# A twelve-stage decoder: the wide cross-attentions' probabilities transposed in 32x32 blocks on VectorE and through DRAM

## The chip, the cores and the metric

The kernel runs on one core of a Trainium2 chip. The metric is device time in microseconds. The three runs shown took 2095.0, 2093.63 and 2095.06 us; their median is 2095.0 us. An engine is named as in the profile: PE is TensorE, DVE VectorE, ACT ScalarE, POOL GpSimd, SP SyncE (here it only issues DMAs).

## The reference

The program is a decoder of four layers. Each layer adds an attention, a cross-attention to a context and a feed-forward block to x, each on a layer norm of x. The batch is 4, the sequence 256, the width 128; the context has 512 tokens of width 96. All of it is float32. The two cross-attentions of the first and the last layer (stages X0 and X3) are wide: 16 heads of 64 features. Cut to what matters, both compute

```python
q = split(x_norm @ Wq)            # (4, 16, 256, 64)
k, v = split(ctx @ Wk), split(ctx @ Wv)   # (4, 16, 512, 64)
p = softmax(q @ k.T * 64 ** -0.5)  # (4, 16, 256, 512)
x = x + merge(p @ v) @ Wo + b
```

X0 adds low-rank terms to its weights, and keeps the last 4 context tokens apart, with a softmax of their own. Its long softmax runs over the other 508. The other stages are a one-head attention, a small grouped attention with a mixture of experts (F0), three more attentions and cross-attentions, a gated feed-forward, a feed-forward with 4-bit rounding (ffn2), and at the end six layers of local attention with a feed-forward (F3).

## The kernel before, in words

The four batch elements are almost independent, so the stages of different batch elements overlap. A list `ORDER` says in which sequence the pieces of the stages are written down. The class `Flow` then makes the real order. Every step is an operation with an engine, a cost in us and a due-time offset (the tables `NET` and `LOCAL`), the buffers that it reads, writes or holds, and the steps that it needs. `Flow.order` is a list scheduler: at each turn it takes, among the operations that can start first, the one with the earliest due time, and so fixes the order of the instructions on each of the five engines. Buffers have a fixed number of slots (`Net.TILES`, all cut from one SBUF arena by `LAYOUT`), and eight PSUM banks. Where the plan has PE waiting over 0.7 us for a bank's work, it puts in filler transposes of the identity (`keep`), 0.7 of the gap at 0.11 us each. The offsets and the paces in these tables are plain numbers in the source; all of them differ between the two kernels, so that the order of all stages differs somewhat.

X0 and X3 are written by `cross_wide` (lines 623 to 646). Per batch element `pair_values` makes the values of all heads: 8 products `p_v` of 512 columns, copied out of PSUM alternately by DVE (`p_vout`) and ACT (`p_vout_a`). `causal_wide` (stage A2) uses `pair_values` too, with 4 products per batch element. Then `cross_pair` runs for each of 8 pairs of heads:

- `p_k`, `p_q`: keys and queries of the pair on PE, copied out on ACT (`p_kout`) and DVE (`p_qout`).
- For each half t of the 256 queries: `p_scores` (PE, two banks, one for each head e), and per head `p_max` (DVE, line 687), `p_exp` (ACT, line 689), `p_recip` (DVE, line 691) and `p_share` (POOL, line 694, division by the sum).
- For each half and head: `p_turn`, four 128x128 transposes on PE into a bank (line 413 is the helper that issues them), and a copy of the bank into the tile `pT`, on ACT for t = 0 (`p_pT_a`) and on DVE for t = 1 (`p_pT`). Line 418 is the helper of all these copies.
- `p_weigh`: 8 products of PE with the values, keys on the partitions, and `p_wout` (ACT).

After 8 pairs `pair_out` projects and adds to x. There are 2 stages x 4 batch elements x 8 pairs = 64 pairs, 128 halves and 256 groups of four transposes.

PE, DVE, ACT and POOL each run their instructions in the planned order. SP issues the weight loads (`fetch`) in its planned order; a load that must wait for its buffer holds back what stands behind it. The weights of F3 are issued by ACT.

Of the kernel before, what the change touches and what calls it, by code (L numbers as in the profile page):

```python
# [22 lines left out]
F32 = mybir.dt.float32  # L23
# [323 lines left out]
class Net:  # L347
# [11 lines left out]
        "im": (384, 1), "xin": (256, 2), "h": (256, 2), "h2T": (256, 2), "rtmp": (256, 3), "gates": (16, 2),  # L359
        "top": (16, 6), "tr": (2, 6), "ss": (16, 2), "qs": (48, 4), "row": (128, 3),  # L360
        "pad0": (256, 2), "pad8": (256, 2), "vs": (1040, 2), "vb": (576, 2),
# [4 lines left out]
    w4 xT kx qx nmx sums p pT big st mv rs xn  # L366
    """

    def __init__(self, ctx, d):
# [14 lines left out]
            ("bank", *LocalBlock.TILES), ("scores", "weigh"), PORT, after,  # L384
        )
        self.flow.keep = lambda b: self.transpose(b.t[:, :P], d.ident)
        self.n = 0
# [214 lines left out]
    def pair_values(self, b, w, src, reads, chunks):  # L602
# [3 lines left out]
        for h in range(2):  # L606
            for c in range(chunks):
# [5 lines left out]
                self.evac("p_vout_a" if c % 2 else "p_vout", lambda to=to, at=at: to.t[:, at : at + 512],  # L613
# [45 lines left out]
    def cross_pair(self, b, g, w, xT, v, vmade, vt, oT, n, image):  # L659
# [12 lines left out]
        nmx, sums, pT, halves = self.buf("nmx"), self.buf("sums"), self.buf("pT"), []  # L672
        for t in range(2):
# [8 lines left out]
            for e in range(2):  # L682
# [23 lines left out]
                tp, half = self.buf("bank"), Buffer()  # L706
                halves.append(half)

                def turn(cols=cols, tp=tp):
                    for c in range(4):  # L710
                        self.transpose(tp.t[:, c * P : (c + 1) * P], cols(lo=c * P, hi=(c + 1) * P))

                self.op("p_turn", turn, [prob], [tp], [pT, p])
                self.evac(
                    "p_pT" if t else "p_pT_a",
                    lambda e=e, t=t: pT.t.rearrange("p (e c q) -> p e c q", e=2, q=S)[:, e, :, t * P : (t + 1) * P],
                    lambda tp=tp: tp.t.rearrange("p (c q) -> p c q", q=P), [tp], [half], [pT],
                )
        po, out = self.buf("bank"), Buffer()

        def weigh():
            pT4 = pT.t.rearrange("p (e c q) -> p e c q", e=2, q=S)
            for c in range(4):
                for e in range(2):
                    self.mm(
                        po.t[64 * e : 64 * (e + 1), :S], v(c, (2 * g + e) * 64), pT4[:, e, c, :], c == 0, c == 3
                    )

        self.op("p_weigh", weigh, [*halves, *vmade], [po], [pT, *vt, oT])
        self.evac("p_wout", lambda: oT.t[:, g * S : (g + 1) * S], lambda: po.t[:, :S], [po], [out], [oT])  # L730
        return out

# [1546 lines left out]
def slots():  # L2279
    return {"bank": 8} | {k: n for t in (Net.TILES, LocalBlock.TILES) for k, (_, n) in t.items()}  # L2280
# [4 lines left out]
    "n_stats": ("DVE", 0.77, -12.92),  # L2285
    "n_stats4": ("DVE", 1.36, 286.90),
    "n_eps": ("DVE", 0.11, -13.72),
    "n_root": ("POOL", 0.74, 139.58),
    "n_scale": ("DVE", 0.55, -1.32),
    "n_scale4": ("DVE", 1.18, 108.13),  # L2290
    "n_turn": ("PE", 0.25, 1.55),
    "warm": ("PE", 0.1, -281.88),
    "load_a": ("SP", 0.8, -912.31),
    "load_x": ("SP", 0.55, -820.02),
    "load_low": ("SP", 0.3, -687.28),
    "load_ups": ("SP", 2.05, -698.37),
    "load_wk": ("SP", 1.55, -609.16),
    "load_ctx0": ("SP", 0.8, -534.64),
    "load_wv": ("SP", 1.55, -493.10),
    "load_wq": ("SP", 2.05, -382.27),  # L2300
    "load_ctx": ("SP", 0.8, -269.42),
    "load_rows": ("SP", 1.55, -258.50),
    "load_image": ("SP", 1.55, -199.31),
    "load_wo": ("SP", 2.05, -147.00),
    "load_mask": ("SP", 0.9, 29.11),
    "k_causal": ("POOL", 1.4, 36.07),
    "k_ident": ("DVE", 0.2, -1.98),
    "k_masks": ("POOL", 1.7, 18.24),
    "k_pads": ("POOL", 1.3, 6.33),
    "k_values": ("POOL", 2.4, -15.88),  # L2310
    "k_image": ("POOL", 1.3, -15.31),
    "k_pick": ("POOL", 3.1, 50.17),
    "n_out": ("ACT", 0.34, 4.37),
    "add": ("DVE", 0.45, 12.29),
    "fetch": ("SP", 0.3, -129.69),
    "h_qk": ("PE", 0.87, -14.62),
    "h_qkout": ("DVE", 0.82, -17.26),
    "h_v": ("PE", 0.7, -17.34),
    "h_vout": ("ACT", 0.4, -209.49),
    "h_scores": ("PE", 0.87, -365.48),  # L2320
    "h_max": ("DVE", 0.74, -137.84),
    "h_exp": ("ACT", 1.0, 8.08),
    "h_recip": ("DVE", 0.1, 26.91),
    "h_turn": ("PE", 0.45, -7.58),
    "h_pT": ("ACT", 0.56, -83.79),
    "h_weigh": ("PE", 0.9, 4.47),
    "h_add": ("DVE", 0.64, -161.75),
    "p_v": ("PE", 0.92, -1.50),
    "p_vout_a": ("ACT", 0.62, -51.76),
    "p_vout": ("DVE", 0.63, 9.55),  # L2330
    "p_out": ("PE", 3.8, -8.71),
    "p_k": ("PE", 0.86, -1.76),
    "p_kout": ("ACT", 0.61, -23.45),
    "p_kimg": ("POOL", 0.22, -160.23),
    "p_q": ("PE", 0.45, 0.36),
    "p_qout": ("DVE", 0.36, -5.17),
    "p_scores": ("PE", 0.86, -7.16),
    "p_max": ("DVE", 0.62, -0.59),
    "p_exp": ("ACT", 0.71, 8.17),
    "p_recip": ("DVE", 0.1, 2.43),  # L2340
    "p_share": ("POOL", 0.73, -151.14),
    "p_img": ("DVE", 0.13, -114.70),
    "p_turn": ("PE", 0.47, -12.59),
    "p_pT": ("DVE", 0.63, 7.21),
    "p_pT_a": ("ACT", 0.62, -130.20),
# [400 lines left out]
```

## Time and profile before

| | us |
|---|---|
| median of three runs | 2095.0 |
| profiled execution, first to last instruction (span) | 2090.2 |
| PE busy (PE's weight loads busy) | 2027.3 (1354.4) |
| DVE busy | 1620.6 |
| ACT busy | 1176.6 |
| POOL busy | 991.7 |
| DMA traffic, MB | 71.20 |

The page gives no other time for the profiled execution than its span; the runs' median is 4.8 us above it. The mean granted clock of TensorE is 0.989. Busy time is the union of an engine's instructions. Matmul records overlap, since the next one starts while the last is still in flight, so a busy PE isn't a PE at its peak, and the cost of one matmul in a row of them is the distance between starts. The time by stretch is the better view: X0 lies between 34 and 362 us, X3 between 931 and 1230 us, and F3 behind.

### The profile page before, as it was taken

To read this page: it belongs to the slowest core of one execution; us is meant where nothing else is said; L and a number is where in the kernel's file an instruction comes from. 1 tells how busy PE (TensorE), PEld (TensorE's weight loads), DVE (VectorE), ACT (ScalarE), POOL (GpSimd) and SP (SyncE) were. 2 spreads that over 40 slices of the span, in tenths; PEclk is the share of its full clock that TensorE was granted. 3 is DMA by queue.
4 is the path that set the end of the run, shared out by engine and by line. 5 is a ranking of instruction groups with operands and counts; after the bars stand their busy time and mean duration, and the time that the engine had idled before them with its cause. 6 is when DMAs were issued, how large, how long until landed. Compare 5 with 4: busy or idle time off the path is not lost.

```text
span 2090.2 us, 59652 instructions
## 1 busy us (share of the span) xinstructions
PE 2027.3 (97%) x24411; PEld 1354.4 (65%) x24411; DVE 1620.6 (78%) x4281; ACT 1176.6 (56%) x2668; POOL 991.7 (47%) x1155
## 2 busy tenths in 40 slices
PE   9999999999999998999999999999999999999998
PEld 5656676776675666666556656666666666566666
DVE  6676877698786769988886589789787797797882
ACT  4565636344536677666656555555655565556553
POOL 4343424231312236444474367557566575575660
PEclk8999999999999999999999999999999999999999
DMA  5000020111020000100000101121121021111101
GB/s 158 1 1 1 1 71 1 42 42 45 5 74 2 9 1 25 39 1 1 1 1 1 52 21 63 46 70 46 43 70 43 25 71 53 63 46 42 30 23 32
DMA packets 33328, 71.20 MB, mean 34 GB/s; under 512 B 5528, under 2 KB 17888, under 8 KB 33056
## 3 DMA queue, kind: packets, MB, share of 16 engines
q1 hardware_dynamic: 20816, 51.48, 8.4%
q10 hardware_dynamic: 12240, 15.91, 2.3%
q8 instruction: 193, 3.16, 0.6%
q14 instruction: 79, 0.65, 0.1%
HBM read 41.69 MB, written 0.52 MB: 20 GB/s over the span
## 4 chain that ended last, share of the span: by engine, by line
PE 70%; DVE 20%; POOL 5%; issue 3%; ACT 1%; DMA 0%; SPq 0%; POOLq 0%; ACTq 0%; DVEq 0%
PE bank L410 40%; PE bank L1844 17%; PE bank L413 9%; PE bank L2060 2%; DVE arena L1998 2%; DVE arena L2008 2%; DVE arena L2013 2%; POOL arena L2050 1%; POOL arena L2012 1%; DVE arena L1637 1%; POOL arena L2093 1%; PE bank L2134 1%; DVE arena L2101 1%; DVE arena L2103 1%; DVE arena L2033 1%
## 5 line engine op out<-in xcount | busy, mean ns | idle before, releaser
L410 PE MATMUL bank<-arena 128*64 128x256 f32 (+12 forms) x6824 | 853.9, 393 | 6.6 <-ACT arena L1558 2.6
L410 PEld LDWEIGHTS bank<-arena 128*128 128x128 f32 (+5 forms) x6824 | 530.3, 165 | 269.1 <-issue 91.1
L1844 PE MATMUL bank<-arena 64*64 64x32 f32 (+3 forms) x13584 | 651.0, 251 | 6.8 <-issue 3.8
L1844 PEld LDWEIGHTS bank<-arena 64*64 64x64 f32 (+2 forms) x13584 | 386.8, 127 | 208.6 <-issue 115.7
L418 ACT COPY arena<-bank 128x256 f32<-128x256 f32 (+4 forms) x586 | 269.7, 489 | 273.6 <-PE bank L410 183.9
L2012 POOL TENSOR_TENSOR arena<-arena 128x1024 f32<-128x1024 f32 x96 | 226.5, 2363 | 124.3 <-PE bank L1844 65.1
L694 POOL TENSOR_SCALAR arena<-arena 128x508 f32<-128x508 f32 (+1 forms) x256 | 175.7, 693 | 214.3 <-DVE arena L691 189.4
L413 PE MATMUL bank<-ident,arena 128*128 128x128 f32 (+1 forms) x1757 | 252.2, 279 | 18.3 <-DVE arena L457 7.3
L413 PEld LDWEIGHTS bank<-ident,arena 128*128 128x128 f32 (+1 forms) x1757 | 194.7, 141 | 116.1 <-issue 41.3
L689 ACT ACTIVATE arena<-bank,arena 128x508 f32<-128x508 f32 (+1 forms) x256 | 174.7, 690 | 74.7 <-DVE arena L687 41.7
L2050 POOL TENSOR_TENSOR arena<-arena 128x1024 f32<-128x1024 f32 x96 | 180.6, 1902 | 74.0 <-DVE arena L2034 74.0
L2006 ACT ACTIVATE arena<-bank 128x512 f32<-128x512 f32 x192 | 114.2, 602 | 135.6 <-PE bank L1844 108.3
L687 DVE TENSOR_REDUCE arena<-bank 128x1 f32<-128x508 f32 (+1 forms) x256 | 163.8, 676 | 21.5 <-PE bank L410 21.3
L993 ACT ACTIVATE arena<-bank 128x512 f32<-128x512 f32 (+1 forms) x256 | 125.3, 580 | 72.8 <-PE bank L410 71.4
L2008 DVE TENSOR_TENSOR arena<-bank,arena 128x512 f32<-128x512 f32 x192 | 127.7, 683 | 37.7 <-ACT arena L2006 35.2
L418 DVE COPY arena<-bank 128x512 f32<-128x512 f32 (+1 forms) x196 | 125.4, 665 | 39.3 <-PE bank L413 26.6
L1998 DVE TENSOR_TENSOR arena<-bank,arena 128x256 f32<-128x256 f32 x384 | 138.5, 411 | 1.4 <-ACT arena L2006 1.4
L2093 POOL TENSOR_TENSOR arena<-arena 128x1024 f32<-128x1024 f32 x48 | 91.3, 1902 | 99.7 <-ACT arena L2066 62.7
L970 DVE TENSOR_REDUCE arena<-bank 128x1 f32<-128x512 f32 (+2 forms) x256 | 116.2, 513 | 22.6 <-PE bank L410 22.1
L2066 ACT COPY arena<-bank 128x512 f32<-128x512 f32 x192 | 103.3, 603 | 30.5 <-PE bank L2060 30.5
L2060 PEld LDWEIGHTS bank<-ident,arena 128*128 128x128 f32 x768 | 88.1, 143 | 41.9 <-POOL arena L2050 23.4
L2060 PE MATMUL bank<-ident,arena 128*128 128x128 f32 x768 | 102.1, 279 | 13.3 <-POOL arena L2050 13.3
(228 smaller groups left out, 2417.3 us busy)
## 6 DMA issues: line engine op xcount, KB each, us to landing
arena<-arena SPq DMA_DIRECT2D x48, 384.0 KB, 3.8
arena<-in_f_w SPq DMA_DIRECT2D x24, 512.0 KB, 3.5
arena<-in_f_wqkv ACTq DMA_DIRECT2D x18, 512.0 KB, 6.8
arena<-arena SPq DMA_DIRECT2D x48, 128.0 KB, 2.7
arena<-in_f_wo ACTq DMA_DIRECT2D x6, 512.0 KB, 4.0
arena<-in_f_w ACTq DMA_DIRECT2D x6, 341.0 KB, 4.0
arena<-in_f_w ACTq DMA_DIRECT2D x6, 192.0 KB, 5.9
arena<-in_x_wq SPq DMA_DIRECT2D x2, 512.0 KB, 3.3
```

What stands on the lines that cost most here:

```text
L410: self.nc.tensor.matmul(out, lhsT, rhs, start=start, stop=stop)
L413: self.nc.tensor.transpose(out, in_, self.d.ident)
L418: return self.op(name, lambda: copy(out(), in_()), reads, writes, holds)
L687: self.op("p_max", lambda ps=ps, one=one: nc.vector.tensor_reduce(one(nmx), ps.t[:, :n], AX.X, ALU.max, negate=True), [ps], [most], [nmx])
L689: self.op("p_exp", lambda ps=ps, one=one, cols=cols: nc.scalar.activation(cols(), ps.t[:, :n], AF.Exp, bias=one(nmx), accum_out=one(sums)) ...
L694: nc.gpsimd.tensor_scalar(cols(), cols(), one(sums), 1.0, ALU.mult, ALU.mult)
L1844: self.nc.tensor.matmul(out, lhsT, rhs, start=start, stop=stop)
L1998: nc.vector.tensor_mul(heads(tmp.t[:, cut])[:, :, lo : lo + 32], heads(ps.t)[:, :, 32 - lo : 64 - lo], spread(1, lo, lo + 32),)
L2008: op("cosine", lambda cut=cut, ps=ps: nc.vector.tensor_mul(heads(out.t[:, cut]), heads(ps.t), spread(0, 0, 64)), [ps, w["tab"]], [out])
L2012: op("rotary", lambda: nc.gpsimd.tensor_add(out.t, out.t, tmp.t), [out, tmp], [out])
L2050: nc.gpsimd.tensor_mul(heads(out.t), heads(out.t), rs.t[:, at : at + 16, None].to_broadcast([P, 16, 64]))
L2060: nc.tensor.transpose(ps.t[:, i * P : (i + 1) * P], out.t[:, (g + i) * P : (g + i + 1) * P], d.ident)
```

## The change

In `cross_pair` the transposes on PE and the copies of their banks go. In their place:

- `p_turn` (now DVE, one per half, 128 in all): `nc.vector.transpose` of 128x1024 probabilities, both heads of a half. It transposes every 32x32 block in itself and writes the blocks in another order into a new tile `ts`. A block's keys then lie on 32 partitions, but on the 32 of the queries' block, not on their own.
- `p_send` (SP, one per pair): four DMAs of 32 partitions each, 256 KB, from `ts` into a room in DRAM, which put each row where it belongs.
- `p_move` (SP, one per pair): one DMA of 1 MB from the room back into `pT`.
- `p_weigh` reads `pT` by a strided pattern in runs of 32 elements.

There are three rooms in DRAM (`ROOMS`) and two `ts` tiles of 8 KB per partition. To make space, `xin` goes from two slots to one and `rtmp` from three to two (both are used by F0 alone). All value copies of `pair_values` go to ACT, those of A2 too. The planner counts 3.5 us from the end of `p_send`, and 6.0 us from the end of `p_move`, until their data have landed. All due-time offsets, both paces and both patiences are new; the costs of the steps that stay are the same.

```diff
-        "im": (384, 1), "xin": (256, 2), "h": (256, 2), "h2T": (256, 2), "rtmp": (256, 3), "gates": (16, 2),
+        "im": (384, 1), "xin": (256, 1), "h": (256, 2), "h2T": (256, 2), "rtmp": (256, 2), "gates": (16, 2),
...
+        "ts": (2048, 2), "pad0": (256, 2), "pad8": (256, 2), "vs": (1040, 2), "vb": (576, 2),
...
+        self.rooms = [dram.tile([P, 2048], F32, tag=f"room{i}", name=f"room{i}", bufs=1) for i in range(ROOMS)]
...
-                self.evac("p_vout_a" if c % 2 else "p_vout", lambda to=to, at=at: to.t[:, at : at + 512],
+                self.evac("p_vout_a", lambda to=to, at=at: to.t[:, at : at + 512],
...
-                tp, half = self.buf("bank"), Buffer()
-                halves.append(half)
-
-                def turn(cols=cols, tp=tp):
-                    for c in range(4):
-                        self.transpose(tp.t[:, c * P : (c + 1) * P], cols(lo=c * P, hi=(c + 1) * P))
-
-                self.op("p_turn", turn, [prob], [tp], [pT, p])
-                self.evac(
-                    "p_pT" if t else "p_pT_a",
-                    lambda e=e, t=t: pT.t.rearrange("p (e c q) -> p e c q", e=2, q=S)[:, e, :, t * P : (t + 1) * P],
-                    lambda tp=tp: tp.t.rearrange("p (c q) -> p c q", q=P), [tp], [half], [pT],
-                )
+                probs.append(prob)
+            turned.append(self.blocks_turned(p, ts, t, probs[-2:]))
+        self.blocks_moved(ts, turned, pT)
...
-            pT4 = pT.t.rearrange("p (e c q) -> p e c q", e=2, q=S)
+            pT4 = pT.t.rearrange("p (a t e c i) -> p e c t a i", a=4, t=2, e=2, c=4)
...
-        self.op("p_weigh", weigh, [*halves, *vmade], [po], [pT, *vt, oT])
+        self.op("p_weigh", weigh, [pT, *vmade], [po], [*vt, oT])
...
+    def blocks_turned(self, p, ts, t, reads):
+        nc, done = self.nc, Buffer()
+        self.op("p_turn", lambda: nc.vector.transpose(
+            ts.t.rearrange("p (m t x i) -> p t m x i", m=4, t=2, i=32)[:, t],
+            p.t.rearrange("p (x m i) -> p m x i", m=4, i=32)), reads, [done], [p, ts])
+        return done
+
+    def blocks_moved(self, ts, turned, pT):
+        nc, room, sent = self.nc, self.fixed("room", self.rooms), Buffer()
+
+        def send():
+            to, from_ = room.t.rearrange("(m j) (a x) -> a j m x", m=4, a=4), ts.t.rearrange("p (m x) -> p m x", m=4)
+            for a in range(4):
+                nc.sync.dma_start(out=to[a], in_=from_[32 * a : 32 * (a + 1)])
+
+        self.op("p_send", send, turned, [sent], [ts, room])
+        self.op("p_move", lambda: nc.sync.dma_start(out=pT.t, in_=room.t), [sent], [pT], [room])
...
-    "p_turn": ("PE", 0.47, -12.59),
-    "p_pT": ("DVE", 0.63, 7.21),
-    "p_pT_a": ("ACT", 0.62, -130.20),
-    "p_weigh": ("PE", 1.62, 27.56),
+    "p_turn": ("DVE", 1.17, -1174.67),
+    "p_send": ("SP", 2.2, -26.91),
+    "p_move": ("SP", 0.55, 962.30),
+    "p_weigh": ("PE", 1.62, 22.74),
...
-NET_PACE = 1.197514
-NET_PATIENCE = 10.319527
+NET_PACE = 1.220588
+NET_PATIENCE = 6.798603
...
-LOCAL_PACE = 1.123621
-LOCAL_PATIENCE = 0.000000
+LOCAL_PACE = 1.128757
+LOCAL_PATIENCE = 6.287785
...
-LAGS = {**{k: 2.0 for k in NET if k[:5] == "load_"}, "fetch": 6.0, "constants": 4.0, "weights": 12.0, "spread": 3.5}
+LAGS = {**{k: 2.0 for k in NET if k[:5] == "load_"}, "fetch": 6.0, "p_send": 3.5, "p_move": 6.0, "constants": 4.0, "weights": 12.0, "spread": 3.5}
...
+ROOMS = 3
```

## The prediction

> **What bounds the kernel now.** I read the page's busy times and slices first, then the busy time by stretch, then the time line of TensorE around the transposes, and last the groups by shape and the DMA issues.
>
> ```profile
> span 2090.2 us, 59652 instructions
> PE 2027.3 (97%) x24411; PEld 1354.4 (65%) x24411; DVE 1620.6 (78%) x4281; ACT 1176.6 (56%) x2668; POOL 991.7 (47%) x1155
> PE 70%; DVE 20%; POOL 5%; issue 3%; ACT 1%; DMA 0%; SPq 0%; POOLq 0%; ACTq 0%; DVEq 0%
> ```
>
> TensorE is busy nearly always and holds 70% of the chain that ended last; no DMA is on that chain. The first and the last row maximum of each wide cross-attention (line 687) start at 34.0 and 361 us and at 931 and 1229 us, so I cut the span there:
>
> ```profile
> 0.00:34.00 34.00, 29.89 (x132) 20.40 (x134) 16.36 (x47) 6.78 (x15) 15.77 (x43) 0.80 0.85 242
> 34.00:362.00 328.00, 328.00 (x2312) 214.47 (x2310) 237.65 (x775) 190.86 (x494) 130.11 (x336) 1.00 0.04 12
> 362.00:931.00 569.00, 555.54 (x5064) 382.72 (x5062) 450.17 (x1451) 320.42 (x873) 186.52 (x304) 1.00 0.08 26
> 931.00:1230.00 299.00, 291.51 (x1758) 180.99 (x1755) 239.04 (x617) 181.62 (x475) 142.21 (x185) 0.99 0.03 10
> ...
> 800.00:850.00 50.00, 44.91 (x339) 31.76 (x338) 46.99 (x161) 33.82 (x114) 29.03 (x44) 1.00 0.10 28
> ```
>
> After the stretch and its length the columns are PE, PEld, DVE, ACT, POOL, the clock, DMA share and GB/s. In both cross-attention stretches PE is full (328 of 328, 291.5 of 299) and DVE comes next with 238 and 239. The last line shows how full DVE gets anywhere here: 47.0 of 50, 0.94. DMA is almost unused there, 3 to 4%.
>
> ```profile
> 1143.13 1.47 PE L413 MATMUL bank<-ident,arena 128*128 128x128 f32 x12
> 1144.53 3.86 PE L410 MATMUL bank<-arena 64*128 64x512 f32 x24
> 1148.33 1.53 PE L413 MATMUL bank<-ident,arena 128*128 128x128 f32 x12
> 1149.79 0.48 PE L410 MATMUL bank<-arena 64*128 64x128 f32 x2
> ```
>
> Twelve transposes hold PE from 1143.13 to 1144.53 and twelve more from 1148.33 to 1149.79: 2.86 us for 24, a slot of 0.119 us each (the 279 ns of one is latency that the next overlaps).
>
> ```profile
> L418 DVE COPY arena<-bank 128x512 f32<-128x512 f32 x184 | 120.8, 682 | 37.6 <-PE bank L413 26.6 <-PE bank L410 10.3
> L2013 DVE TENSOR_REDUCE arena<-arena 128x16 f32<-128x1024 f32 x96 | 114.3, 1200 | 0.0
> L1506 DVE TENSOR_TENSOR arena<-arena 128x1024 f32<-128x1024 f32 x4 | 5.1, 1274 | 6.0 <-POOL arena L1505 6.0
> L2050 POOL TENSOR_TENSOR arena<-arena 128x1024 f32<-128x1024 f32 x96 | 180.6, 1902 | 74.0 <-DVE arena L2034 74.0
> arena<-arena SPq DMA_DIRECT2D x48, 384.0 KB, 3.8
> arena<-in_f_w SPq DMA_DIRECT2D x24, 512.0 KB, 3.5
> arena<-arena SPq DMA_DIRECT2D x48, 128.0 KB, 2.7
> arena<-in_ctx SPq DMA_DIRECT2D x4, 192.0 KB, 2.6
> ```
>
> These give the prices: a 128x512 copy out of PSUM costs DVE 120.8/184 = 0.657 us, a pass over 128x1024 in SBUF 1.2 us. A DMA needs 2.6 to 2.7 us when small, plus 2.9 us per MB (192 to 512 KB) or 4.3 us per MB (128 to 384 KB).
>
> **The change part by part.**
>
> *TensorE, removed.* 2 stages x 4 batches x 8 pairs x 4 groups of 4 transposes = 1024 slots of 0.119 = 122 us. The order of the instructions in the two built programs puts 124 of the 256 groups inside the first stretch and 122 inside the second: 59 and 58 us. So PE alone would need 328 - 59 = 269 and 299 - 58 = 241 us. The other 10 groups (5 us) lie where PE bounds too.
>
> *VectorE, removed and added.* The 128 copies p_pT go, and p_vout (40 of the 80 value copies, eight of them in A2) moves to ScalarE. By the order 62 + 12 = 74 and 60 + 13 = 73 copies leave the stretches: 48.6 and 48.0 us. 61 and 62 block turns come in. No row shows this operation. Its nearest rows are the reduction (1.2) and the two-input pass (1.27) over the same 128x1024 on the same engine; I take 1.2. The ends are 1.06 (ScalarE's exponential over 128x1024, line 2105) and 1.9 (the same size on POOL). DVE becomes 237.65 - 48.6 + 73.2 = 262 and 239.04 - 48.0 + 74.4 = 265 us. That is 97% of PE's 269 and more than PE's 241. At the 0.94 of the fullest slice the stretches need 279 and 282 us. **DVE takes over the bound in both**, and instead of 117 us they give back 627 - 561 = 66. What is late next there is the row maximum, so the scores wait for banks. With the turn at 1.06 they give 84, at 1.27 56.
>
> *Work moved by the new due times.* The order has 14 more p_v inside the two stretches and as many fewer outside (two matmul records of 0.46 us each, 0.92): 13 us of PE leave parts that PE bounds and enter stretches where PE now has room. The rest that moves is smaller (four expert passes, four projections of the last stage); I leave it at 0, bounds -10 and +10, as for the reordered start and last stage.
>
> *ScalarE* loses 128 copies and gains 40 of about 0.56 us (L418's rows there): 49 us less on an engine at 56 to 61%. Nothing, hidden beside PE and DVE; without that cover it would be a gain.
>
> *SP and DMA.* Per pair four sends of 256 KB to DRAM, then one 1 MB load back that waits for them: 320 issues of about 0.45 us, 144 us on SP, which computes nothing. 128 MB at the 285 GB/s of the start (242 at share 0.85) is 450 us of DMA in 561 us, beside compute. The trip: the sends 5 to 6.5 us, the load 5 to 6.5, in sum 10 to 13. What stands behind a waiting load on SP are next sends and the weights of F0 and A1, fetched ahead; a delay of some 5 us is hidden by that lead. The trip itself must be covered by PE's order. From the second p_scores of a pair to its p_weigh the order holds 17.8 us of PE work on average (14.9 to 35.8, mean 18.9 in stage 0; 11.2 to 30.8, mean 16.8 in stage 3; 12.7 on average before), in the code's cost per step, which where I compared fits the rows (p_max 0.62; three of line 687 take 1.86). The chain it covers is two maxima 1.24, exponential 0.9 (with reading its sum), reciprocal 0.15, share 0.7, turn 1.2, hand-overs 0.6, thus 4.8, plus the trip: 15 to 18. At 17 the pairs that are short add to 50 us; about 2.2 pairs are in flight and a pause counts for all of them, so 23 us of pauses. They lie inside the 51 us that PE idles anyway when DVE bounds, so they add 0 (0 to 20).
>
> *Fillers.* The order has 365 filler transposes against 210: 155 x 0.119 = 18 us, in those pauses: 0 in the sum, 18 if PE alone bounds.
>
> *Buffers.* xin goes from 2 to 1 and rtmp from 3 to 2, to make room. Each serves F0 alone; a later f_turns waits for a POOL addition of 0.8 us: 0 to 10 us, hidden under DVE's other work; I take 0. The strided right operand of p_weigh: 0 (to 10 us, 512 matmuls at 0.02).
>
> **Sum** against the profiled execution: -66 - 13 - 5 = -84, so a span of 2006. The runs' median, 2095.0, is 4.8 above the span of 2090.2; I leave that unchanged: **2011 us**.
>
> **A rule against the change.** The row says 0.119 us for a transpose on TensorE, and a DVE pass of 1024 elements 1.2 us. The Trainium skill, "VectorE: DVE Perf Modes", The three transpose paths, has 390 ns for a 128x128 bf16 transpose on TensorE and 311 ns on VectorE, and its rules for authors send a 128x128 transpose to TensorE where PSUM will do. By its 311 ns a turn of eight such tiles is an estimated 2.5 us, and the stretches would come out some 85 us longer than 645 us, thus slower. In streaming PE the row is a third of the page's figure, and a lone tile's price includes a start that one long instruction pays once, so I stay with the rows.
>
> **The rivals.**
> - *PE alone still ends it*: the work is mixed so well that DVE never holds PE. For it: PE still has more work than DVE over the first 1230 us (about 1110 against 980). Against it: the order moves little between stretches. -122 + 18 = -104: 1991.
> - *The trip is too long*: at 15 us instead of 12 (DMAs of SP queueing among themselves) the short pairs add to 185 us, 84 with 2.2 in flight: 510 + 84 = 594, -33 - 18 = -51: 2044. It would be slower only from about 17 us. Against it: the rows' 10 to 13.
> - *The turn is dear* (the other side): DVE without turns holds 380 us in the two stretches; 123 turns at x, over 0.94, reach the old 627 + 18 us at x = 1.84. At 1.9 it is 653: +8, 2103; at 2.36 (POOL's slowest 128x1024, line 2012) +68, 2163. For it: no row of this operation, and its output is strided. Against: DVE's two 128x1024 rows.
> - *Nothing changes* in the 4 us (0.2%) that a measurement of this kernel can tell: only by gain and turn cancelling near x = 1.84.
>
> **How the numbers follow.** Forecast 0.52 (its own range 1985 to 2040), PE alone 0.17, long trip 0.14 (a quarter of it past its turning point), dear turn 0.14, cancelled 0.03. Faster: 0.52 + 0.17 + 0.10 = 0.79; same 0.03; slower 0.04 + 0.14 = 0.18. The range goes from below the PE case (1991 less the 15 us of moved work) to the dear turn's near end: 1975 to 2100, with about 0.05 below and 0.14 above.
>
> **What would show it.** The helper's transposes on PE should fall by 1024 less the 155 fillers; DVE in the two stretches should be at 0.9 or more and PE at about 0.9; a turn should last 1.2 us; the load back should land in 5 to 6.5 us and PE's wait for it stay under 25 us. I am wrong if the turn is over 1.8 us, if PE's waits name the load, or if the middle and last stretches move by more than 20 us.

## The result, and the profile after

The changed kernel takes 2125.07 us (median of four runs, 2120.37 to 2128.79); the kernel before took 2094.32 us beside it. The ratio is 1.0161, with a 95% interval of 1.0136 to 1.0187: 1.6% slower, where 2011 us and a gain were forecast. The profiled execution took 2120.37 us, its span is 2118.6 us.

First the page of the changed kernel: span, PE's and DVE's busy time, and the chain of work that ended last.

```profile
span 2118.6 us, 58103 instructions
PE 1969.9 (93%) x23542; PEld 1265.3 (60%) x23542; DVE 1664.9 (79%) x4241; ACT 1133.6 (54%) x2580; POOL 993.0 (47%) x1155
PE 46%; DVE 29%; DMA 11%; POOL 5%; issue 4%; ACT 3%; SPq 2%; ACTq 0%; POOLq 0%; DVEq 0%
```

PE was relieved (97% before, 93% now), and DVE hasn't filled up in its place (79%). What is new is DMA with 11% of the chain, where it had 0%.

The stretches of the changed kernel, cut at the first and last row maximum of X0 and X3 (the columns are those of the prediction: stretch, length, PE, PEld, DVE, ACT, POOL, clock, DMA share, GB/s):

```profile
31.00:370.00 339.00, 308.48 (x1921) 181.91 (x1918) 264.56 (x768) 171.50 (x458) 130.25 (x335) 0.97 0.65 207
370.00:922.00 552.00, 533.17 (x4918) 363.00 (x4917) 437.23 (x1442) 316.24 (x865) 185.60 (x306) 0.99 0.10 33
922.00:1259.00 337.00, 288.30 (x1401) 149.66 (x1400) 276.68 (x617) 168.90 (x440) 151.27 (x188) 0.94 0.62 195
```

X0 went from 327 to 338 us and X3 from 297 to 336, from first to last maximum. Neither engine is full there: PE has 308 of 339 and 288 of 337, DVE 0.78 and 0.82. The middle got shorter (569 to 552). The span's 28.4 us are +11 in X0, +39 in X3, -17 in the middle, and -4 at the start and the end.

What PE, DVE and SP waited for in the changed kernel (us in total, times, longest; `room` is the DRAM buffer, line 745 the load back, 742 the sends, 730 the turn):

```profile
PE bank L412 <- DMA arena<-room: 63.0, 29, 8.2
PEld bank L412 <- DMA arena<-room: 26.8, 11, 4.1
DVE arena L730 <- DMA room<-arena: 18.1, 11, 4.7
SPq L745 <- DMA room<-arena: 263.3, 113, 7.2
```

PE stood 63.0 + 26.8 = 90 us at `p_weigh` for the load back. DVE stood 18 us because `ts` was not yet sent. SP stood 263 us at loads until their own sends had landed.

The turn, and the issues of the two DMA steps with KB each and the median us to landing:

```profile
L730 DVE STREAM_TRANSPOSE arena<-arena 128x1024 f32<-128x1024 f32 x128 | 157.0, 1234 | 20.5 <-DMA room<-arena 18.1
room<-arena SPq DMA_DIRECT2D x256, 256.0 KB, 6.5
arena<-room SPq DMA_DIRECT2D x64, 1024.0 KB, 6.3
```

SP's queue in X0 of the changed kernel, as a time line (start, us that the issues took, line):

```profile
66.06 0.34 SPq L745 DMA_DIRECT2D arena<-room  x1
66.45 2.52 SPq L742 DMA_DIRECT2D room<-arena  x4
74.80 0.34 SPq L745 DMA_DIRECT2D arena<-room  x1
75.18 2.51 SPq L742 DMA_DIRECT2D room<-arena  x4
83.85 0.34 SPq L745 DMA_DIRECT2D arena<-room  x1
```

Four sends take 2.5 us to issue (66.45 to 68.97), SP then waits 5.8 us until they have landed, issues the load at 74.80, and only then the sends of the next pair. One pair goes through in about 9 us, and while the load of one pair runs, the sends of the next run beside it.

Over all 64 pairs, the time from the second turn's end to the first send is 1.95 us on average (the sends stand behind the previous pair's waiting load), from the first send to the load's issue it is 8.42, and the load takes 6.3 (median): **the trip is 16.7 us**. The planner had counted on 2.2 + 3.5 + 0.55 + 6.0 = 12.25, I on 10 to 13.

### The profile page after: what moved, and what is told of

Its sections match the earlier page's. It is cut to its first block, busy times and chain, and to the rows that moved or that the text cites. A ratio compares the mean times of both kernels' runs of the same rounds, so it can differ in the third digit from the quotient of the medians.

```text
span 2118.6 us, 58103 instructions
## 1 busy us (share of the span) xinstructions
PE 1969.9 (93%) x23542; PEld 1265.3 (60%) x23542; DVE 1664.9 (79%) x4241; ACT 1133.6 (54%) x2580; POOL 993.0 (47%) x1155
## 4 chain that ended last, share of the span: by engine, by line
PE 46%; DVE 29%; DMA 11%; POOL 5%; issue 4%; ACT 3%; SPq 2%; ACTq 0%; POOLq 0%; DVEq 0%
PE bank L412 28%; PE bank L1858 11%; DMA room<-arena 6%; DMA arena<-room 4%; PE bank L415 4%; DVE arena L2012 3%; DVE arena L2022 3%; DVE arena L2027 3%; PE bank L2074 2%; DVE arena L730 2%; SPq L742 2%; DVE arena L690 2%; DVE arena L2117 2%; DVE arena L2115 2%; POOL arena L2064 1%
## 5 line engine op out<-in xcount | busy, mean ns | idle before, releaser
L412 PE MATMUL bank<-arena 128*128 128x128 f32 (+10 forms) x6824 | 885.2, 402 | 88.9 <-DMA arena<-room 63.0
L412 PEld LDWEIGHTS bank<-arena 32*128 32x128 f32 (+5 forms) x6824 | 536.8, 167 | 384.3 <-issue 137.3
L1858 PE MATMUL bank<-arena 64*64 64x32 f32 (+2 forms) x13584 | 647.7, 250 | 14.1 <-issue 9.0
L1858 PEld LDWEIGHTS bank<-arena 64*64 64x64 f32 (+2 forms) x13584 | 382.1, 126 | 204.5 <-issue 130.9
L420 ACT COPY arena<-bank 128x256 f32<-128x256 f32 (+3 forms) x498 | 224.4, 472 | 315.1 <-PE bank L412 271.8
L730 DVE STREAM_TRANSPOSE arena<-arena 128x1024 f32<-128x1024 f32 x128 | 157.0, 1234 | 20.5 <-DMA room<-arena 18.1
L415 PE MATMUL bank<-ident,arena 128*128 128x128 f32 (+2 forms) x733 | 126.5, 288 | 19.1 <-POOL arena L1656 6.2
L415 PEld LDWEIGHTS bank<-ident,arena 128*128 128x128 f32 (+2 forms) x733 | 83.0, 143 | 82.8 <-issue 19.3
L2027 DVE TENSOR_REDUCE arena<-arena 128x16 f32<-128x1024 f32 x96 | 114.8, 1206 | 0.2
```

The source lines that it names most:

```text
L412: self.nc.tensor.matmul(out, lhsT, rhs, start=start, stop=stop)
L415: self.nc.tensor.transpose(out, in_, self.d.ident)
L420: return self.op(name, lambda: copy(out(), in_()), reads, writes, holds)
L730: self.op("p_turn", lambda: nc.vector.transpose(ts.t.rearrange("p (m t x i) -> p t m x i", m=4, t=2, i=32)[:, t], p.t.rearrange("p (x m i) ...
L1858: self.nc.tensor.matmul(out, lhsT, rhs, start=start, stop=stop)
L2027: op("norms", lambda: nc.vector.tensor_reduce(ss.t[:, at : at + 16], heads(sq.t), AX.X, ALU.add), [sq], [ss])
```

## The experiments

Three theories were set against each other: the trip theory (PE waits because the trip through DRAM is too long, by its bytes or by its latency), the DVE theory (the forecast's: DVE bounds the two stages), and the order theory (the new due times cost the time). "X0 + X3" below is the sum of both stages from first to last row maximum: 624.6 us before, 674.2 in the changed kernel. A pair's *cover* is the PE work that the order holds from its second scores to its weighing. A pair's *chain* is what the cover has to hide, from the first row maximum of its second half to the landed load.

### The same DMAs with 32 columns each

```diff
-                nc.sync.dma_start(out=to[a], in_=from_[32 * a : 32 * (a + 1)])
+                nc.sync.dma_start(out=to[a][:, :, :32], in_=from_[32 * a : 32 * (a + 1), :, :32])
-        self.op("p_move", lambda: nc.sync.dma_start(out=pT.t, in_=room.t), [sent], [pT], [room])
+        self.op("p_move", lambda: nc.sync.dma_start(out=pT.t[:, :32], in_=room.t[:, :32]), [sent], [pT], [room])
```

> The changed kernel in its own order, with the same 320 DMAs, but each send and each load back carries 32 columns instead of 512 or 2048, so nearly no bytes (most of the probabilities aren't moved, so the output is left incomplete; the two pT tiles are cleared once at the start). Trip theory (PE waits for the way through DRAM, about 14.8 us from the first send to the landed load): the trip falls to about 7 us, PE's 90 us of waits on the load vanish, the two stretches go from 676 to about 565 us, and the time is 2010 to 2030 us. DVE theory (the forecast's: DVE bounds the stretches): DVE's work is unchanged, the stretches stay near 676 us, 2110 to 2125. Order theory (the new due times cost it): 2110 to 2125 too.

Measured: 2035.86 us, ratio to before 0.9732 (0.9713 to 0.9752). No wait of PE names the room. The two stretches of this run:

```profile
34.00:336.00 302.00, 299.82 (x1927) 176.55 (x1924) 264.15 (x768) 171.18 (x458) 130.22 (x335) 1.00 0.13 35
885.00:1178.00 293.00, 278.69 (x1416) 143.81 (x1416) 274.71 (x615) 168.25 (x442) 149.78 (x187) 0.98 0.11 24
```

The order, the instructions and the buffers are those of the changed kernel; 89 us are gone, and of the 83 us by which the profiled span fell, 80 are in X0 (301) and X3 (293). DVE has the same work as in the changed kernel (264 and 275 us), so neither DVE nor the order as such explains the loss. X0 is now full on PE (300 of 302) and X3 has DVE at 275 of 293, the 0.94 of the forecast.

The edit takes away more than the bytes, though. The 32 columns belong to the pair's first half alone, so the sends no longer stand behind the second turn: in 62 of 64 pairs they start before it has ended, in the changed kernel in none. The trip cost 89 us in this order, by its bytes and by its place behind the second turn together.

### Half of the bytes

```diff
-            for a in range(4):
+            for a in range(2):
-        self.op("p_move", lambda: nc.sync.dma_start(out=pT.t, in_=room.t), [sent], [pT], [room])
+        self.op("p_move", lambda: nc.sync.dma_start(out=pT.t[:, :1024], in_=room.t[:, :1024]), [sent], [pT], [room])
```

> The changed kernel in its own order, with two sends of 256 KB and a load of 512 KB per pair (half of the probabilities aren't moved; the pT tiles are cleared once). Trip theory, by bytes: the DMA rings are shared by one pair's send and the last pair's load, 2 MB per 8.5 us; with half the bytes the send lands in 4 to 5 instead of 6.5 us and the load in 4 to 4.5 instead of 6.3, trip about 9.5 us, time 2030 to 2060. Trip theory, by latency (a landing takes its 6 us whatever it carries): send and load land in 5.5 to 6.5 us each, time 2095 to 2115. DVE theory: 2110 to 2125.

Measured: 2033.07 us, ratio 0.9719 (0.97 to 0.9739); X0 + X3 592.5 us. Sends land in 3.6 us, loads in 3.9, and the load is issued 4.9 us after the first send on average: a trip of 8.8 us, and nothing is left of the loss. Here every pair's sends still stand behind its second turn, as in the changed kernel, so the length of the trip is enough to explain the loss. The cost isn't in proportion to the bytes. Somewhere between a trip of 8.8 and one of 16.7 us it begins.

### Longer trip in the plan

```diff
-"p_send": 3.5, "p_move": 6.0,
+"p_send": 6.4, "p_move": 6.4,
```

> The changed kernel, but the planner is told of the measured landings (6.4 us each instead of 3.5 and 6.0), so that it puts more PE work between a pair's scores and its p_weigh. Order theory in the form that the plan only misjudged the trip: PE's waits on the load go from 90 to under 30 us and the time to 2060 to 2085. Trip theory by bytes: two tiles of each kind and the shared rings still allow a pair only every 8.7 us, so the waits move to other places and the time stays within 2100 to 2125. DVE theory: no change, 2115 to 2125.

Measured: 2120.42 us, ratio 1.0123 (1.0097 to 1.0148). X0 + X3 fell by 31 us to 643.2, and PE's wait from 90 to 68 us, but X3's end to the end of the kernel took 889 us instead of 860, and the middle 561 instead of 552. PE's and SP's waits for the trip:

```profile
PE bank L412 <- DMA arena<-room: 42.2, 24, 2.9
PEld bank L412 <- DMA arena<-room: 25.3, 12, 3.2
SPq L745 <- DMA room<-arena: 40.7, 24, 4.9
```

By the total the new plan seemed worthless; by the stages it helped where it should, and the other stages came out longer. The reading is that the list scheduler, whose due times were fitted to the old lags, put them in a worse order; the runs with due times fitted anew, below, bear on that. The new plan also changed SP's order: 52 of the 64 loads now stand behind a later pair's sends, where 8 did, and SP's wait at the loads fell from 263 to 41 us. The trip got no shorter by it (0.04 + 10.45 + 8.06 = 18.5 us, the same three parts as above), and PE still waited.

### Without DRAM: 16 DMAs per pair from SBUF to SBUF

```diff
             for a in range(4):
-                nc.sync.dma_start(out=to[a], in_=from_[32 * a : 32 * (a + 1)])
-
-        self.op("p_send", send, turned, [sent], [ts, room])
-        self.op("p_move", lambda: nc.sync.dma_start(out=pT.t, in_=room.t), [sent], [pT], [room])
+                for m in range(4):
+                    nc.sync.dma_start(
+                        out=pT.t[32 * m : 32 * (m + 1), a * 512 : (a + 1) * 512],
+                        in_=ts.t[32 * a : 32 * (a + 1), m * 512 : (m + 1) * 512],
+                    )
+
+        self.op("p_send", send, turned, [pT], [ts])
...
-    "p_send": ("SP", 2.2, -26.91),
-    "p_move": ("SP", 0.55, 962.30),
+    "p_send": ("SP", 7.2, -26.91),
...
-"p_send": 3.5, "p_move": 6.0,
+"p_send": 2.5,
```

> The blocks go from SBUF to SBUF in one hop: 16 DMAs of 64 KB per pair straight into pT, no DRAM, no second DMA, half the bytes; the planner counts 7.2 us of issue and 2.5 us to landing. Trip theory: the trip is 16 issues of 0.45 = 7.2 plus a landing of 2.3 to 2.7, thus 9.5 to 10 us instead of 14.8; the time is 2020 to 2060. DVE theory: 2110 to 2125. If SP's issue rate binds instead (16 x 0.45 x 32 = 230 us per stretch, or 0.65 to 1.2 each under load as some sends show), 2060 to 2110.

Measured: 2258.8 us, ratio 1.0793 (1.0769 to 1.0818). The DMA issues, and PE's first wait:

```profile
arena<-arena SPq DMA_DIRECT2D x1024, 64.0 KB, 2.0
```

```profile
PE bank L412 <- DMA arena<-arena: 143.8, 48, 5.7
```

Half of the bytes and a landing of 2.0 us, and yet the slowest of all: 16 issues in a row take SP 10.4 us, 0.65 us each, more than a pair's share of a stage (X0's 301 us without trip / 32 = 9.4). Between one pair's last issue and the next pair's first there are 0.11 us (median), and SP's queue holds 19% of the chain that ended last: the trip is bound by its issues here. That is a miss of mine (0.45 us each was assumed), and it says nothing on DRAM itself. A second thing differs: with a trip of 9.7 us in the plan the order holds only 15.0 us of cover per pair, less than any other run with all pairs moved, and the two causes aren't separated.

### Every second pair by the old way

```diff
+                if g % 2:
+                    tp, half = self.buf("bank"), Buffer()
+                    halves.append(half)
...
+                    self.op("p_tturn", turn, [prob], [tp], [pT, p])
...
-        self.blocks_moved(ts, turned, pT)
+        if not g % 2:
+            self.blocks_moved(ts, turned, pT)
...
+    "p_tturn": ("PE", 0.47, -12.59),
+    "p_pT": ("DVE", 0.63, 7.21),
+    "p_pT_a": ("ACT", 0.62, -130.20),
```

> Every second pair goes the old way (transposes on PE, copies on ACT and DVE with the costs and due offsets of before), the others the new way, so the bytes of the trips halve and each trip has two pairs' time. Trip theory: the waits of PE for the load fall from 90 us to under 20; PE has 61 us more of transposes than with all pairs moved, DVE 64 turns less (79 us) and 64 copies more (42 us). Without the bytes the kernel took 2036 us with DVE at 0.94 in X3 and PE full in X0; with half of the transposes back on PE I expect 2040 to 2060, faster than before. DVE theory (the turn is what costs): DVE's work falls by 37 us, so at most that much of 2125 is gained: about 2090. Order theory (the new due times cost the time): little changes, 2100 to 2125.

Measured: 2115.76 us, ratio 1.0116 (1.0093 to 1.0139). PE waits 1.3 us for the load. X0 + X3 is 630.7 us, 43 less than in the changed kernel and 6 more than before, but from X3's end to the kernel's end it takes 898 us (2107.9 - 1210), where the changed kernel has 860:

```profile
1210.00:2300.00 1090.00, 845.62 (x15333) 577.73 (x15328) 676.96 (x1388) 469.97 (x803) 514.29 (x288) 0.99 0.14 39
```

The two stages lost the wait, and the rest came out longer, as in the run with the longer trip planned.

### The load back issued by ScalarE's queue

```diff
-        self.op("p_move", lambda: nc.sync.dma_start(out=pT.t, in_=room.t), [sent], [pT], [room])
+        self.op("p_move", lambda: nc.scalar.dma_start(out=pT.t, in_=room.t), [sent], [pT], [room])
...
-    "p_move": ("SP", 0.55, 962.30),
+    "p_move": ("ACT", 0.55, 962.30),
...
-"p_send": 3.5, "p_move": 6.0,
+"p_send": 6.4, "p_move": 6.4,
```

> The load back is issued from ScalarE's queue instead of SyncE's, with 6.4 us planned for the sends and for the load, so that no send and no weight load stands behind a waiting load on SyncE. If the bytes on the DMA rings make the trip long, it stays at 2100 to 2125 us, as with the same planned times on SyncE (2120), with some us more for ScalarE's waiting at the loads. If it is the waiting on SyncE that holds the next pair's sends back, sends and loads overlap more and it comes to 2060 to 2090.

Measured: 2096.14 us, ratio 1.0031 (1.0011 to 1.0051). The total lies between the two expectations, so the stages have to decide. Against the run with the same planned times on SP it is 24 us less, but X0 + X3 is 651.8 instead of 643.2: the gain lies in the other stages' order (854 us from X3's end instead of 889, the middle 553 instead of 561). A queue of its own for the load did not make the two stages shorter. PE's wait for the load fell (44 us against 68), but now ScalarE's exponentials (line 692) stood behind loads that waited for their sends:

```profile
ACT arena L692 <- DMA room<-arena: 39.1, 9, 8.0
```

### A turn of a quarter of the size, with the 32-column trip

```diff
-            ts.t.rearrange("p (m t x i) -> p t m x i", m=4, t=2, i=32)[:, t],
-            p.t.rearrange("p (x m i) -> p m x i", m=4, i=32)), reads, [done], [p, ts])
+            ts.t.rearrange("p (m t x i) -> p t m x i", m=4, t=2, i=32)[:, t, :, :2],
+            p.t.rearrange("p (x m i) -> p m x i", m=4, i=32)[:, :, :2]), reads, [done], [p, ts])
```

> As the run with 32 columns per DMA, but the block turn also covers only a quarter (128 x 256 of 128 x 1024); the rest of the turned tile is left as it is, so most of the turning and moving is left out. A turn should fall from 1.23 to about 0.4 us, DVE's work in each stretch by some 50 us. If DVE bounded X3 there (275 us of work in 293, 0.94) and PE bounded X0 (300 of 302), X3 falls to 265 to 280 (then PE ends it) and X0 stays at 295 to 301; the whole 2010 to 2030 us. If DVE bounds both, both fall by over 15 us. If neither, both stay within 4 us, and 2036 stays.

Measured: 2024.2 us, ratio 0.9677 (0.9644 to 0.971); a turn takes 0.432 us. The two stretches of this run:

```profile
34.00:332.00 298.00, 296.93 (x1916) 174.37 (x1913) 216.58 (x765) 170.37 (x456) 129.55 (x334) 1.00 0.14 35
882.00:1167.00 285.00, 273.06 (x1404) 141.39 (x1403) 231.40 (x616) 168.36 (x441) 149.57 (x188) 0.99 0.11 24
```

DVE has 48 and 43 us less to do, X0 falls by 3.0 us (300.7 to 297.7) and X3 by 9.0 (293.2 to 284.2), less than the 13 or more that were expected. So PE bounds X0. In X3 DVE was the bound at 0.94, but PE stood 9 us behind it.

### The new order with the old transposes

```diff
-            turned.append(self.blocks_turned(p, ts, t, probs[-2:]))
-        self.blocks_moved(ts, turned, pT)
+                    self.op("p_tturn", turn, [prob], [tp], [pT, p])
+                    self.evac(
+                        "p_pT" if t else "p_pT_a",
...
```

> The due times, paces, buffers and ScalarE's value copies of the changed kernel, but every pair transposed on PE and copied as before (costs and due offsets of those steps as before): no turn and no trip. It shows what the new order costs or gives by itself. Trip theory: as before or somewhat better, 2075 to 2100, since the stretches outside of X0 and X3 were 17 us shorter in the changed kernel and this remains. Order theory: the new due times hold the 30 us that the changed kernel lost, so 2115 to 2130.

Measured: 2140.12 us, ratio 1.0242 (1.0211 to 1.0273), slower than both kernels, with X0 + X3 at 650.4 us and 891 us from X3's end to the kernel's end (861 before, 860 in the changed kernel). Taken alone it would speak for the order theory. But the 32-column run and the half-of-the-bytes run have the changed kernel's very order and are fast, so that order isn't bad for the steps that it was fitted to. That it is bad for other steps is the likely reading, not a shown one; a run that swaps steps under fixed due times measures the misfit as well.

### Every second pair, due times fitted to it

The due-time offsets, paces and patiences were fitted anew to the steps of the run with every second pair, for the shortest plan of the kernel's own scheduler. For example:

```diff
-    "p_send": ("SP", 2.2, -26.91),
-    "p_move": ("SP", 0.55, 962.30),
+    "p_send": ("SP", 2.2, -151.99),
+    "p_move": ("SP", 0.55, 894.43),
...
-NET_PATIENCE = 6.798603
+NET_PATIENCE = 14.805498
```

> The kernel that moves every second pair, with due-time offsets, paces and patiences fitted anew to its own steps; nothing else differs from the run with every second pair. There X3 to the end took 898 us against 860 in the changed kernel and 861 before, with no wait on a trip, so its loss lay in the order of the other stages. Trip theory: with an order that fits, the 61 us of transposes that PE no longer does show: 2045 to 2075 us, PE's wait for loads under 15 us. If mixing the two ways costs by itself (DVE's share, banks), it stays above 2090.

Measured: 2064.15 us, ratio 0.9866 (0.9852 to 0.9881), inside the range of the trip theory. PE waits 0.4 us for loads. But the gain isn't where that theory had it: X0 + X3 is 621.3 us, only 3 us less than before, though 61 us of transposes left PE. The rest of the gain lies in the middle (559 us against 569) and from X3's end to the kernel's end (847 against 861). So the total was met in part by luck. What the run does show is that due times fitted to the steps bring the last part from 898 to 847 us.

### All pairs moved, a longer trip planned, due times fitted to it

```diff
-    "p_turn": ("DVE", 1.17, -1174.67),
-    "p_send": ("SP", 2.2, -26.91),
-    "p_move": ("SP", 0.55, 962.30),
+    "p_turn": ("DVE", 1.17, -1093.93),
+    "p_send": ("SP", 2.2, 2.98),
+    "p_move": ("SP", 0.55, 808.47),
...
-"p_send": 3.5, "p_move": 6.0,
+"p_send": 7.0, "p_move": 9.0,
```

(and the other offsets, the paces and the patiences; no step, buffer or DMA differs from the changed kernel.)

> The changed kernel with all pairs through DRAM, but with 7.0 us planned for the sends and 9.0 us for the load (3.5 and 6.0 before), and with due-time offsets, paces and patiences fitted anew to these. The bytes stay. Trip theory in its form 'too long for the order': PE finds other work during the trip, its wait for loads falls from 90 to under 30 us, and with DVE at 0.94 in X3 and PE near full in X0 the whole is 2040 to 2075 us. If instead the bytes bound the stretches by themselves (two passes at the 8.8 to 9.15 us from load to load that the changed kernel shows, 32 pairs, so 282 to 293 us per stage, plus the weights' loads), PE's wait for loads stays over 60 us whatever is planned, X0 and X3 stay over 320 us, and the whole is 2090 to 2125 us.

Measured: **2046.87 us, ratio 0.9778 (0.9762 to 0.9795)**. Every byte of the trip is moved, and the kernel is 2.2% faster than before. Of the 39 us by which its profiled span is shorter, 33 are in X0 + X3 (591.6 against 624.6). Its stretches, in the same columns:

```profile
34.00:331.00 297.00, 293.44 (x1871) 168.43 (x1867) 257.88 (x755) 166.31 (x447) 128.95 (x331) 1.00 0.72 230
894.00:1189.00 295.00, 275.68 (x1427) 146.79 (x1427) 268.10 (x603) 164.44 (x436) 147.87 (x186) 0.99 0.68 218
```

Its waits for the trip, of PE and of SP, and its DMA issues:

```profile
PE bank L412 <- DMA arena<-room: 5.7, 5, 1.9
SPq L745 <- DMA room<-arena: 36.4, 27, 6.1
```

```profile
room<-arena SPq DMA_DIRECT2D x256, 256.0 KB, 6.0
arena<-room SPq DMA_DIRECT2D x64, 1024.0 KB, 7.9
```

The trip is no shorter: 0.28 + 10.76 + 7.9 = 18.9 us, against 16.7. It is covered. PE has 23.5 us of work from a pair's second scores to its weighing, against 17.8 (in the order of the built programs, at the code's cost per step). SP's time line shows what else differs from the changed kernel:

```profile
106.45 3.48 SPq L742 DMA_DIRECT2D room<-arena  x4
110.04 0.85 SPq L745 DMA_DIRECT2D arena<-room  x1
112.46 3.39 SPq L742 DMA_DIRECT2D room<-arena  x4
116.02 0.52 SPq L745 DMA_DIRECT2D arena<-room  x1
```

The load at 110.04 follows the sends of the next pair with no wait, since it belongs to the pair sent before. In SP's order 52 of 64 loads stand behind a later pair's sends; in the changed kernel 8 of 64 do, and the others wait for their own. This alone isn't what helped: the run with 6.4 and 6.4 us planned has the same 52 of 64 and nearly the same trip (18.5 us), and PE waited 68 us there. What differs between these two in the trip's favour is the cover, 19.6 against 23.5 us.

### The same with a middling plan, and with the bytes taken away

```diff
-"p_send": 7.0, "p_move": 9.0,
+"p_send": 5.5, "p_move": 7.5,
```

> As the run with all pairs moved and new due times, but with 5.5 us planned for the sends and 7.5 us for the load, and due times fitted to these. In the order of this kernel PE has 20.6 us of work on average from a pair's second scores to its weighing; the changed kernel has 17.8, the run with 6.4 and 6.4 us planned 19.6, the one with 7.0 and 9.0 us 23.5. If it is the cover of the trip that decides, this lies between: PE waits 20 to 50 us for loads, and the whole takes 2060 to 2090 us. If any fitting anew is enough, whatever trip is planned, it takes 2040 to 2055 us as the one with 7.0 and 9.0. If the bytes bound it, over 2090.

Measured: 2075.14 us, ratio 0.9917 (0.9898 to 0.9936), between the two as the cover said: X0 + X3 618.9 us, and of PE's waits

```profile
PE bank L412 <- DMA arena<-room: 32.2, 19, 4.6
PEld bank L412 <- DMA arena<-room: 17.7, 7, 4.8
```

And the plan of 7.0 and 9.0 us with 32 columns per DMA, by the same edit as in the first experiment:

> As the run with all pairs moved and 7.0 and 9.0 us planned (2047 us), in the same order, but each DMA of the trip moves 32 columns instead of 512 or 2048, so most of the moving is left out. If the longer cover hides the trip, taking its bytes away saves little: 2035 to 2047 us. If the bytes still cost in that order, it falls to 2000 to 2030 us.

Measured: 2042.91 us, ratio 0.977 (0.9749 to 0.9791), X0 + X3 588.9 us. Here too the sends start ahead of the second turn's end, so the edit can only take away more than the bytes. In the order that covers the trip this gains 4 us, which the two intervals don't tell from nothing; in the order of the changed kernel it gained 89.

| run | planned trip | chain | PE's cover | cover with fillers | PE waits for load | X0 + X3 | total |
|---|---|---|---|---|---|---|---|
| changed kernel | 12.25 | 23.5 | 17.8 | 18.8 | 89.8 | 674.2 | 2125.1 |
| 6.4 and 6.4 planned | 15.55 | 24.7 | 19.6 | 21.4 | 67.5 | 643.2 | 2120.4 |
| the same, load on ScalarE's queue | 15.55 | 25.7 | 20.5 | 22.5 | 44.1 | 651.8 | 2096.1 |
| 5.5 and 7.5, refitted | 15.75 | 24.0 | 20.6 | 22.3 | 49.9 | 618.9 | 2075.1 |
| 7.0 and 9.0, refitted | 18.75 | 25.0 | 23.5 | 25.1 | 6.2 | 591.6 | 2046.9 |
| half of the bytes, changed kernel's order | 12.25 | 15.6 | 17.8 | 18.8 | 0.7 | 592.5 | 2033.1 |
| 32 columns, changed kernel's order | 12.25 | 9.6 | 17.8 | 18.8 | 0 | 593.9 | 2035.9 |

(The planned trip is 2.2 + 0.55 us of issues and the two lags. Chain and cover are means over the pairs, the chain over the 44 to 50 whose load's landing the trace has; the fillers are counted at the 0.119 us of a transpose. The wait adds PE's and its weight loads'.) With both steps on SP's queue, PE's wait and the two stages follow what the chain has over the cover: both are small where the cover, with its fillers, is at least as long as the chain. The run with the load on ScalarE's queue is out of line, and there ScalarE stands too. The total follows where the rest of the order fits. What isn't settled: whether the kernel before would also gain from another order; none was run.

## Why the prediction was wrong

**The step that failed** is "*SP and DMA*": "The trip: the sends 5 to 6.5 us, the load 5 to 6.5, in sum 10 to 13", and what was built on it, pauses of 23 us that "lie inside the 51 us that PE idles anyway when DVE bounds, so they add 0 (0 to 20)". Three things were wrong in it.

- *Its length.* The single landings were priced well at the upper end (6.5 and 6.3). Two pieces were left out: the issue of four sends in a row (2.5 us before the last is under way, so that the first send and the load's issue are 8.42 us apart), and the sends' waiting behind the previous load (1.95). 16.7 us came out. The part ahead of the trip was short as well: from the first maximum of a pair's second half to the end of its turn the trace has a median of 6.4 us, not 4.8. So the chain was 23 us against a cover of 17.8, where 15 to 18 were forecast.
- *"a delay of some 5 us is hidden by that lead".* I looked at the weights behind a waiting load, not at the next pair's sends. Those are what stood there, in 56 of 64 loads, so the trips followed one another. That alone doesn't explain PE's waits: in the run with 6.4 and 6.4 us planned 52 of the 64 loads had the later sends ahead of them, and PE still waited 68 us.
- *That pauses of PE disappear in idle time.* PE takes its steps in order. While it stands at `p_weigh`, the next scores stand behind it, so DVE's maxima come late too, and DVE's share fell to 0.78 and 0.82 instead of holding 0.94. 90 us of waiting went with 83 us of span (2118.6 against 2035.4 with 32 columns): most of it was not hidden.

The Trainium skill, "DMA: Bandwidth & Descriptors", Anatomy of one DMA — SWDGE (gpsimd) path, has 2.0 us plus the bytes over 436 GB/s for one DMA on GpSimd's path, an estimated 4.4 us for 1 MB, and says that a wait on a semaphore is served by the issuing sequencer before it dispatches. SP's 263 us at the loads are the second of these. For the first, the run with every second pair comes near with 4.8 us, on SP's queue; where all pairs moved the same load took 6.3 us in the changed kernel, with the next pair's sends beside it, and up to 8.1 in the runs with a longer planned trip. So a price of one DMA by itself was a lower end here.

**The rival "the trip is too long"** named the mechanism, and was undervalued. It gave 2044 us at a trip that ends the chain later by 3 us, since it let the pauses replace DVE's bound, and put the turning point at 17 us. Its own sum, short pairs over 2.2, gives 272 / 2.2 = 123 us for a chain of 21.5 us (4.8 + 16.7; 272 us is what the pairs of the order lack together), against 83 measured. Even so it would have ended at 510 + 123 = 633 and about 2083 us, still a gain, because its base of 510 us for the two stretches was too low as well: with the trip empty they took 594.

**What was right.**
- The counts: the helper's transposes on PE fell from 1757 to 733, by 1024, and fillers rose from 230 to 385, by 155.
- The turn: 1.234 us against 1.2, so the dear turn fell. The estimate of 2.5 us from the Trainium skill, "VectorE: DVE Perf Modes", The three transpose paths, is twice the 1.234 us of the row; the measurement decides.
- DVE's work: 265 and 277 us against 262 and 265. As the bound at 0.94 it appeared in X3 once the trip was empty (274.7 of 293), though only by 9 us; where the trip was covered DVE stood at 0.91 (268.1 of 295), and no run tests whether it bounds there.
- The parts outside of X0 and X3: they lost 21 us together, 17 of them in the middle, where 13 and 5 were forecast. Whether all of that is moved work isn't shown.

**What was right in kind and off in size: the -66.** With the trip empty X0 and X3 take 301 and 293 us, not 279 and 282, and the run took 2036 us, 25 more than the forecast. Of the 113 us by which the span missed 2006, the trip is 83; X0 and X3 without it gave 31 us instead of 66, which is 35; the rest of the kernel gave 24 instead of 18, which takes 6 back. "PE alone would need 269 and 241" left out what the new order brings in. In X0 the other work of this order shows in the groups by shape, of the kernel before first and of the 32-column run second:

```profile
L410 PE MATMUL bank<-arena 128*128 128x256 f32 x168 | 44.5, 385 | 0.0
L410 PE MATMUL bank<-arena 128*128 128x128 f32 x212 | 27.1, 276 | 0.0
L410 PE MATMUL bank<-arena,ctxT 96*128 96x512 f32 x50 | 24.7, 605 | 0.0
```

```profile
L412 PE MATMUL bank<-arena 128*128 128x256 f32 x201 | 51.7, 391 | 0.8 <-ACT arena L420 0.8
L412 PE MATMUL bank<-arena 128*128 128x128 f32 x248 | 32.6, 280 | 0.1
L412 PE MATMUL bank<-arena,ctxT 96*128 96x512 f32 x64 | 30.4, 600 | 0.0
```

These three shapes alone grew by 18.4 us, and 44 fillers added 5.8: together 24 of the 31 us by which PE, at 300, lies over 269. The rest isn't traced to a shape. So DVE never bounded X0. The prediction had counted the `p_v` only as a loss of the stretches outside.

**The clock** was not in the sum. Of the 62 groups of `p_weigh` (16 matmul records) that the trace of X0 and X3 has whole in the changed kernel, 11 took over 3 us, with a median of 1.95. Each of the 11 began right behind a pause of PE of 2.3 to 8.2 us and ran at a granted clock of 0.50 to 0.55; some other pauses of 2.3 to 2.9 us were followed by the full clock. In the run with 7.0 and 9.0 planned it is 1 of 58. The granted clock was 0.97 and 0.94 in the two stretches, and 1.00 and 0.99 there. So a pause for a load often cost a second time here: 11 groups at some 1.65 us more are an estimated 18 us.

## What to carry to other kernels

A step that leaves an engine for a round trip by DMA costs nothing only as long as the order holds enough other work: add the issues, the queue's wait behind the previous trip and the landing beside the next one, and compare that whole chain with the work that the in-order engine has between producer and consumer. Give the planner the trip as it is measured under load, or longer; here taking the trip's bytes away gained 89 us in one order and 4 at most in another. Putting the next item's sends ahead of the previous item's load spares the queue its waits (263 us against 41), but here it wasn't enough: PE waited 68 us with a cover of 19.6 us and 6 us with one of 23.5. Where a scheduler's due times are fitted to the steps, read an experiment by its stages, since a changed step can spoil the order of stages that it has nothing to do with by 30 us.

## What the runs showed of the hardware

- `nc.vector.transpose` of 128x1024 float32 in 32x32 blocks took 1.234 us, as long as a reduction over the same elements (1.2 us), and 0.432 us for 128x256.
- DMAs of 64 KB from SBUF to SBUF cost SP 0.65 us each to issue, 16 in a row; those of 256 KB to DRAM took 0.65 us each in the changed kernel (2.6 us for four, median), and 0.39 where only two stood in a row with half of the bytes. The forecast had 0.45.
- 256 KB sends landed in 4.1 us and the 1 MB load in 4.8 where every second pair moved; where all did, the sends took 5.4 to 6.5 us and the load 6.3 to 8.1 in the runs that issue both from SP (medians of each run).
